# A graph network of two layers on one core: the order of the attention matmuls, their row halves, and the banks of the values behind attention

## The chip, the cores and the metric

The kernel runs on 1 core of one Trainium2 chip. The metric is the device time in microseconds (us) of one execution. TensorE (PE) multiplies matrices with an array of 128 by 128; PSUM is the memory that it writes. VectorE (DVE), ScalarE (ACT) and GpSimd (POOL) work element by element, and SyncE (SP) issues most of the DMAs. Each engine works through its own queue in the order in which its instructions were issued.

## What is computed

Both layers of the network see 8 batches of 2048 nodes with 256 features, all in fp32. Layer 0 is attention in chunks of 256 keys, with the softmax inside each chunk; layer 1 is a graph attention over all nodes. Shortened:

```
h = relu(layernorm(x))
q, k, v = h @ Wq.T + bq, h @ Wk.T + bk, h @ Wv.T + bv      # 4 heads of 64
scores = clip(q . k / sqrt(64), -10, 10), by chunks of 256 keys
scores = where(mask == 0, -10, scores)
ctx = sum over chunks of softmax(scores over the chunk) @ v
x = x + layernorm(ctx @ Wo.T + bo + h) * gamma + beta

h = relu(layernorm(x));  g = h @ W
e = leaky_relu(g @ a1 [rows] + g @ a2 [columns]), -1e9 where adj == 0
x = x + relu(softmax(e) @ g)
```

## The kernel before, in words

**Stages of a batch.** A batch has 4 blocks of 512 nodes, called zero, low, mid and last. Its attention has 32 steps, one for each block of 512 queries and chunk of 256 keys. After them come the rest of the output of layer 0 for the last blocks, the values of layer 1 (`Between.values`, line 843: g and the two scores of each node, from the features `hT`) and the products of layer 1 (`Layer1.products`, line 994). The next batch's q and k (`ahead.qk`, line 447) are made for its first block in steps 32 and 33 of this one, the rest behind attention. Attention of the next batch starts within the last layer-1 products (`early`, lines 581 to 603).

**A step of attention.** The logits of a step are made in four units (`logits`, line 503). A unit is one of the four heads: `ORDER` on line 485 maps a unit to a pair of heads and a row half of the array, the rows 0 to 63 or 64 to 127. Units 0 and 2 work on the upper half (the second 64 rows), units 1 and 3 on the lower. A matmul has 64 rows and 32 columns, so eight of them fit into the array at a time if both halves are used, four if one is. A unit has two halves of four matmuls each, one for each tile of 128 keys (`kt`).

After the logits, VectorE clips and masks a unit (`clip`, line 543), and ScalarE takes the exponential (`exponentials`, line 552). GpSimd adds the two key tiles of a pair of heads (`add`, line 558) into a tile tagged "both", of which there are two buffers. From these the sums of the softmax are made with ones as weights (`sums`, line 531, into ps_t), upper half first and lower half later; the values (`values`, line 519, into two ps_n banks) take the exponentials themselves, half of their matmuls in a first group and half in a later one, one step later. ScalarE inverts the sums (`invert`, lines 563 and 564), VectorE scales the values (`scale`, line 573), and a DMA that GpSimd issues adds the result to the context (`gather`, line 578). Two groups that write one bank of PSUM from different row halves must not run together, so a `fence` (a nop on SyncE, line 475) stands between them: the second waits for a signal that SyncE gives when the first has ended. As SyncE's queue is in order, a DMA behind such a nop is issued after it.

**The order.** It is written by hand (the engines are scheduled manually): `begin(f)` and `end(f)` issue step f, f from 2 to 34, with work from four steps: later values of step f-3, inversion and scale of f-3, logits of f-1, first values and sums of f-2, and the first unit of f. At set half steps (`todo`, keys 2f and 2f+1) other work is called in between: pieces without a mark, and pieces marked "first", "pe", "pe1" or "after" at other places of the step. Half step 65 has the four DMAs that send the turned features of block low (`low.send1`, line 143), half step 67 their fetch (`low.fetch1`, line 155). Half steps 66 and 67 have, for the next batch, q and k of the first block; in the last batch there is no next one, and the values of block zero and the first sources and weights of layer 1 (lines 843, 961 and 971) take their place.

In the kernel before, TensorE's order in `end(f)` and `begin(f)`, f within a batch, is:

```
begin: later values(f-3) | logits(f-1) units 1 and 2
end:   first values(f-2) | unit 3 of f-1 beside upper sums(f-2) | rest of unit 3 beside unit 0 of f
       | lower sums(f-2) beside the rest of unit 0 of f
```

where "beside" means on the other row half. In `early(3)` the first unit of step 1 stands without such a partner. At the end of a batch `last_sums` (in `end(33)`) ends the last step with values and sums mixed.

**PSUM.** It has 2 buffers of two banks (ps_s), 2 of one bank (ps_n) and 2 of one bank (ps_t). ps_s holds logits, ps_n values, ps_t sums. `ps_h` gives one half of a ps_s; `ps_m` gives ps_t, or ps_n and ps_t in turn when `turn_about` says so. Behind the last step the four values of block low go to `ps_h`. Each is copied out by ScalarE (line 851) and VectorE (line 852), and the third needs the buffer of the first.

Of the kernel before, what the change touches and what calls it, by code (L numbers as in the profile page):

```python
# [28 lines left out]
def gnn_two_layers(  # L29
# [29 lines left out]
    KT = CHUNK // P  # L59
# [18 lines left out]
    turn_about = [False, 0]  # L78
# [394 lines left out]
    def fence(before, after):  # L473

        nop = nc.sync.nop()  # L475
        for x in before:
            tc.add_manual_dep(nop.ins, x.ins.name, SYNC, reason="both write one bank of PSUM")
        for x in after:
            tc.add_manual_dep(x.ins, nop.ins.name, SYNC, reason="both write one bank of PSUM")


    class Attention:
# [100 lines left out]
        def early(self, part):  # L583

            if part == 0:
                for kt in range(KT):
                    self.logits(0, 0, kt)
                    self.logits(0, 1, kt)
            elif part == 1:
                for o in range(2):  # L590
                    self.clip(0, o)
                    self.exponentials(0, o)
                for kt in range(KT):
                    self.logits(0, 2, kt)
                    self.logits(0, 3, kt)
            elif part == 2:
                self.clip(0, 2)
                self.exponentials(0, 2)
                self.clip(0, 3)
                self.add(0, 0)  # L600
            if part == 3:
                for kt in range(KT):
                    self.logits(1, 0, kt)

# [3 lines left out]
        def begin(self, f, pieces=()):  # L610

            self.run(pieces, "first")
            if (f - 3, 0) in self.before:
                made = {}
                for kt in range(KT):
                    for half, c in ((0, 0), (1, 1)):
                        made.setdefault(c, []).extend(self.values(f - 3, half, c, kt))
                for c in range(2):
                    fence(self.before.pop((f - 3, c)), made[c])
            if (f - 1, 0) in self.s:  # L620
                self.clip(f - 1, 0)
            if self.has(f - 3):
                self.invert(f - 3)
            if self.has(f - 2):
                self.exponentials(f - 2, 3)
            if self.has(f - 1):
                self.exponentials(f - 1, 0)
            if self.has(f - 3) and not self.has(f - 1):
                self.scale(f - 3, 0)
                self.scale(f - 3, 1)  # L630
            self.run(pieces, "pe")
            if self.has(f - 1):
                for kt in range(KT):
                    self.logits(f - 1, 1, kt)
                    self.logits(f - 1, 2, kt)
                if self.has(f - 3):
                    self.scale(f - 3, 0)
                    self.scale(f - 3, 1)
            if self.has(f - 2):
                self.add(f - 2, 1)  # L640
            if self.has(f - 3):
                self.gather(f - 3)
            self.rest = pieces

        def end(self, f, pieces=()):
            self.run(pieces, "first")
            if self.has(f - 1):
                self.clip(f - 1, 1)
            self.run(pieces, "pe1")
            if self.has(f - 1):  # L650
                self.clip(f - 1, 2)
            self.run(pieces, "after")
            self.run(self.rest, None)
            if self.has(f - 1):
                self.exponentials(f - 1, 1)
                self.exponentials(f - 1, 2)
            if self.has(f - 2):
                made = {}
                for kt in range(KT):
                    for half, c in ((0, 1), (1, 0)):  # L660
                        made.setdefault(c, []).extend(self.values(f - 2, half, c, kt))
                for c in range(2):
                    self.before[f - 2, c] = made[c]
            if self.has(f - 1):
                self.logits(f - 1, 3, 0)
            if self.has(f - 2) and self.has(f - 1):
                sums = self.sums(f - 2, 1)
            if self.has(f - 1):
                self.logits(f - 1, 3, 1)
            if self.has(f):  # L670
                self.logits(f, 0, 0)
            self.run(pieces, None)
            self.run(pieces, "pe")
            if self.has(f - 2) and self.has(f - 1):
                fence(sums, self.sums(f - 2, 0))
            elif self.has(f - 2):
                self.last_sums(f - 2)
            if self.has(f):
                self.logits(f, 0, 1)
            if self.has(f - 1):  # L680
                self.clip(f - 1, 3)
                self.add(f - 1, 0)

        def last_sums(self, n):

            upper = self.sums(n, 1)
            made = {0: self.values(n, 0, 0, 0), 1: self.values(n, 1, 1, 0)}
            made[0] += self.values(n, 0, 0, 1)
            lower = self.sums(n, 0)
            made[1] += self.values(n, 1, 1, 1)  # L690
            for c in range(2):
                fence(self.before.pop((n, c)), made[c])
            fence(upper, lower)

        @staticmethod
        def run(pieces, kind):
# [5 lines left out]
    class Between:  # L702
# [148 lines left out]
            nc.scalar.activation(g[:, at, 0:F], pp[:, 0:F], AF.Copy)  # L851
            nc.vector.tensor_copy(self.sd[:, :, at], pp[:, F:F + 2])

        def ends(self, part):

            if part == 0:
                self.turn1(0)
                self.keep1(0)
                self.turn1(1)
                self.keep1(1)  # L860
            else:
                for t in range(TB):
                    self.values(t)
                    self.keep(t)

        def beside(self, soon):
# [300 lines left out]
    for b in range(B):  # L1167
        sd = small.tile([P, 2, NT], F32, tag="sd", name="sd", bufs=2)
        sums = small.tile([P, NNB, FC], F32, tag="sums", name="sums", bufs=2)
        blocks = [Between(nb, projs[b], att, sd, sums) for nb in range(NNB)]  # L1170
        zero, low, mid, last = blocks
# [24 lines left out]
        if b == 0:  # L1196
# [4 lines left out]
            for nb, ns in enumerate(beats):  # L1201
# [3 lines left out]
                n = ns[-1]  # L1205
# [40 lines left out]
                    piece()  # L1246
        for f in range(2, STEPS + 3):
            if f == STEPS + 2:
                turn_about[:] = [True, 1]
            att.begin(f, todo.pop(2 * f, []))  # L1250
            if unfinished:
                unfinished()
                unfinished = None
            att.end(f, todo.pop(2 * f + 1, []))
# [5 lines left out]
        if ahead:  # L1260
            for t in range(TB):
                mid.stats1([t])
                low.values(t, ps_h)
                low.keep(t)
            low.sum1()
            zero.fetch1()
# [60 lines left out]
            ahead.values(3)  # L1327
        else:
            one.weights(0, 0, range(2, 4), ws[0])
            low.ends(1)  # L1330
            low.sum1()
            one.send(1)
            mid.stats1(range(TB))
# [1 line left out]
            mid.shift1()  # L1335
            accs[0] = one.accumulators(0)
            early(0)
            mid.norm1(0)
            mid.norm1(1)
# [20 lines left out]
            for t2 in range(2):  # L1360
                last.gamma(t2)
                last.add(t2)
            early(1)
            last.stats1(range(TB))
            last.power1()
            last.shift1()
            weights(3)
            last.norm1(0)
            last.norm1(1)
            early(2)  # L1370
            last.ends(0)
            one.total()
# [56 lines left out]
        if ahead:  # L1429
            def unfinished(one=one, acc=accs[NNB - 1]):  # L1430
                one.finish(NNB - 1, acc)
                one.store(NNB - 1)
# [30 lines left out]
```

## Time and profile before

| | |
|---|---|
| time, median of 3 runs | 3520.11 us (3519.66 to 3520.38) |
| profiled execution, its time | 3520.81 us |
| its span | 3519.0 us, granted TensorE clock 1.00 |
| longest groups: clips (L543, VectorE) | 1024 of 1221 ns |
| adds (L558, GpSimd) | 512 of 2419 ns |
| logits (L503, TensorE) | 16384 records of 590 ns, busy 1334.4 us together |
| values (L519, TensorE) | 16384 records of 589 ns, 1120.4 us |
| sums (L531, TensorE) | 4096 records, 548.5 us |
| exponentials (L552, ScalarE) | 1024 of 1049 ns |
| scale (L573, VectorE) | 448 of 687 ns |
| products of layer 1 (L994, TensorE) | 4096 records of about 380 ns |

The span is the time from the first to the last instruction of one profiled execution. A row of a timeline has its start, its duration, the engine, the line of the kernel, the operation, and what is written from what; x32 at its end means that 32 instructions in a row are drawn together. In square brackets stands how long the engine was idle ahead of it, and what it waited for. A matmul in fp32 gives two records, so the 8 matmuls of a unit are 16 records. Records overlap where they work on different tiles of the array, so a busy sum can exceed what the array could do, and a busy TensorE is not a full one. One batch to the next takes 433.9 us (the products' first row in the chain is at 893.25 and then 1327.15).

### The profile page before, as it was taken

Reading aid. Unit: us, or ns where it says so; the run is one execution under the profiler, and the core shown is the slowest. Engines: PE = TensorE matmul, PEld = TensorE weight load, DVE = VectorE, ACT = ScalarE, POOL = GpSimd, SP = SyncE. Lnnn points to the kernel's source line nnn. Section 1 sums busy time; section 2 is a strip of 40 time slices with the busy share of each in tenths; the row PEclk is TensorE's granted clock in tenths of the full one; section 3 lists DMA queues with packets and bytes.
Section 4 is the critical chain, followed back from the end, with each engine's and each line's share of the span. In section 5 each row is a group of like instructions: output and inputs, shape, how many; then the busy total and the mean of one; then the engine's idle time right before and its main releaser. Section 6 shows DMA issues by size and latency. Waiting matters only on the chain.

```text
span 3519.0 us, 104592 instructions
## 1 busy us (share of the span) xinstructions
PE 3499.1 (99%) x46076; PEld 2302.1 (65%) x46076; DVE 2629.9 (75%) x3983; ACT 1959.0 (56%) x2961; POOL 1825.4 (52%) x1198
## 2 busy tenths in 40 slices
PE   9999999999999999999999999999999999999999
PEld 5454775667765577566876758656686655864568
DVE  6887677867678676786767867678686785857876
ACT  6777426763267633676336763367623776147751
POOL 5677017870278702786037850378503784047841
PEclk9999999999999999999999999999999999999999
DMA  7545323443234431444314443244432335124331
GB/s 246 127 109 123 93 88 72 97 108 104 69 86 86 116 102 61 92 92 109 102 61 92 92 105 101 67 92 87 117 106 64 79 85 122 64 55 92 80 77 53
DMA packets 171320, 332.13 MB, mean 94 GB/s; under 512 B 28656, under 2 KB 90352, under 8 KB 170864
## 3 DMA queue, kind: packets, MB, share of 16 engines
q1 hardware_dynamic: 129712, 205.36, 18.5%
q0 software_dynamic: 32832, 119.03, 18.5%
q8 instruction: 360, 5.90, 0.7%
q10 hardware_dynamic: 8320, 1.05, 0.2%
q14 instruction: 96, 0.79, 0.1%
HBM read 156.50 MB, written 51.44 MB: 59 GB/s over the span
## 4 chain that ended last, share of the span: by engine, by line
PE 98%; DVE 1%; ACT 1%; DMA 0%; issue 0%; POOL 0%; SPq 0%; ACTq 0%; DVEq 0%; POOLq 0%
PE ps_s L503 25%; PE ps_n L519 25%; PE ps_s L994 13%; PE ps_t L531 6%; PE ps_n L994 6%; PE ps_t L994 6%; PE ps_t L743 2%; PE ps_t L447 2%; PE ps_n L447 2%; PE ps_s L447 2%; PE ps_n L461 2%; PE ps_t L461 2%; PE ps_n L843 1%; PE ps_t L843 1%; PE ps_s L843 1%; PE ps_n L721 0%
## 5 line engine op out<-in xcount | busy, mean ns | idle before, releaser
L543 DVE SCALAR_TENSOR_TENSOR e<-ps_s,bound 128x1024 f32<-128x1024 f32 x1024 | 1219.2, 1221 | 400.9 <-PE ps_s L503 395.7
L558 POOL TENSOR_TENSOR both<-e 128x1024 f32<-128x1024 f32 x512 | 1222.3, 2419 | 541.9 <-PE ps_t L531 244.7
L503 PE MATMUL ps_s<-q,k 64*32 64x512 f32 x16384 | 1334.4, 590 | 0.2
L552 ACT ACTIVATE e<-e 128x1024 f32<-128x1024 f32 x1024 | 1049.4, 1049 | 456.0 <-DVE e L543 438.3
L519 PE MATMUL ps_n<-e,v 64*32 64x512 f32 x16384 | 1120.4, 589 | 0.0
L503 PEld LDWEIGHTS ps_s<-q,k 64*32 64x32 f32 x16384 | 505.0, 106 | 403.0 <-issue 277.9
L519 PEld LDWEIGHTS ps_n<-e,v 64*32 64x32 f32 x16384 | 522.5, 107 | 365.3 <-issue 266.4
L531 PE MATMUL ps_t<-both,ones 64*32 64x512 f32 x4096 | 548.5, 590 | 0.0
L994 PE MATMUL ps_s<-g,w 128*128 128x257 f32 x2048 | 448.4, 380 | 0.0
L994 PEld LDWEIGHTS ps_s<-g,w 128*128 128x128 f32 x2048 | 388.4, 190 | 56.0
L573 DVE TENSOR_TENSOR prod<-ps_n,rz 128x512 f32<-128x512 f32 x448 | 288.7, 687 | 135.4 <-ACT rz L564 86.5
L1017 POOL TENSOR_TENSOR x<-x,r 128x256 f32<-128x256 f32 x124 | 90.7, 745 | 459.5 <-ACT r L1015 458.7
L977 DVE SCALAR_TENSOR_TENSOR w<-bound,w 128x1024 f32<-128x1024 int8 x256 | 314.7, 1229 | 8.7
L367 POOL TENSOR_TENSOR krn<-krn,mv 128x4 f32<-128x4 f32 x28 | 6.8, 242 | 571.0 <-DVE w L971 571.0
L994 PE MATMUL ps_n<-g,w 128*128 128x257 f32 x1024 | 292.4, 382 | 0.0
L994 PE MATMUL ps_t<-g,w 128*128 128x257 f32 x1024 | 289.7, 380 | 0.0
L563 ACT ACTIVATE rz<-ps_t 128x512 f32<-128x512 f32 x256 | 152.6, 596 | 237.5 <-PE ps_t L531 164.2
L971 DVE TENSOR_SCALAR w<-src,cd 128x512 f32<-128x512 f32 x512 | 263.3, 556 | 19.2 <-ACT src L951 15.3
L994 PEld LDWEIGHTS ps_n<-g,w 128*128 128x128 f32 x1024 | 192.8, 190 | 44.3 <-issue 17.6
L578 POOL DMA_DIRECT2D ctxT<-prod x224 | 192.3, 858 | 56.5 <-DVE prod L573 49.5
L531 PEld LDWEIGHTS ps_t<-both,ones 64*32 64x32 f32 x4096 | 151.9, 106 | 100.6 <-SPq L475 44.4
L994 PEld LDWEIGHTS ps_t<-g,w 128*128 128x128 f32 x1024 | 193.8, 189 | 28.2
(139 smaller groups left out, 2975.8 us busy)
## 6 DMA issues: line engine op xcount, KB each, us to landing
ctxT<-prod POOLq DMA_DIRECT2D x224, 512.0 KB, 5.0
bound<-bound_d SPq DMA_DIRECT2D x125, 512.0 KB, 4.7
turned_d<-squares SPq DMA_DIRECT2D x232, 128.0 KB, 2.9
hT<-turned_d SPq DMA_DIRECT2D x58, 512.0 KB, 4.6
rows<-in_adj_dram SPq DMA_DIRECT2D x32, 512.0 KB, 5.2
x<-in_x_dram SPq DMA_DIRECT2D x32, 512.0 KB, 6.5
out_dram<-x SPq DMA_DIRECT2D x31, 512.0 KB, 2.7
xp<-in_x_dram SPq DMA_DIRECT2D x28, 512.0 KB, 4.4
```

Source lines behind the costliest of these rows:

```text
L447: nc.tensor.matmul(in_key_order(pp) if i == 0 else pp, w[:, di, do * P:(do + 1) * P], h, start=di == 0, stop=di == FC - 1,)
L503: nc.tensor.matmul(self.s[n, o][c * Q:(c + 1) * Q, kt, :], self.k[p][rows, at:at + Q], self.q[p][rows, nb * NB:(nb + 1) * NB], start=True, ...
L519: made.append(nc.tensor.matmul(self.num[n, c][h * Q:(h + 1) * Q, :], self.v[rows, j * KT + kt, at:at + Q], self.e[n, p][rows, i * KT + kt, :],
L531: nc.tensor.matmul(self.total[n][h * Q:(h + 1) * Q, :], ones[rows, :], self.both[n, h // 2][rows, h % 2, :], start=half == 1, stop=half == 0,)
L543: nc.vector.scalar_tensor_tensor(self.e[n, p][:, i * KT:(i + 1) * KT, :], self.s.pop((n, o)), -CLIP * SC, bounds[nb, j // 4][:, j % 4 * KT ...
L552: nc.scalar.activation(e, e, AF.Exp, scale=1.0 / SC)
L558: nc.gpsimd.tensor_tensor(self.both[n, p], e[:, 0], e[:, 1], op=ALU.add)
L573: nc.vector.tensor_tensor(dst[:, c, :], self.num.pop((n, c)), self.rz[n], op=ALU.mult)
L578: nc.gpsimd.dma_start(self.ctxT[nb], self.prod.pop(n), accum_op=ALU.add)
L971: nc.vector.tensor_scalar(w[:, i, :], self.src[nb], self.cd[:, 0, j:j + 1], self.cd[:, 1, j:j + 1], op0=ALU.mult, op1=ALU.max,)
L977: nc.vector.scalar_tensor_tensor(two, bounds1[nb, j // 8][:, j % 8 - 1:j % 8 + 1, :], 0.0, two, op0=ALU.is_gt, op1=ALU.mult)
L994: nc.tensor.matmul(accs[t][:, 0:F + 1], w[:, i, t * P:(t + 1) * P], g[:, j, :], start=j == 0, stop=j == NT - 1,)
```

## The change

The units of a step are now made in the order 1, 0, 3, 2, and those of the next step start before this one is done, a unit sooner than before: within a batch a step has, in this order,

```
begin: later values(f-3) | logits(f-1) units 3 and 2
end:   first values(f-2) | unit 1 of f beside upper sums(f-2) | rest of unit 1 beside unit 0 of f
       | lower sums(f-2) beside the rest of unit 0 of f
```

`early(3)` makes units 1 and 0 of step 1, on both halves, and their clip, and `early(2)` has one exponential more. In step 32, which has no next step, the sums and first values of step 30 stand in `begin` ahead of the rest of unit 2; in step 33 the sums and first values of 31 stand ahead of the pieces of the step (k of the next batch, or the sources of layer 1) and the later values behind them. `sums_and_values` puts upper sums, first values and lower sums in a row; `last_sums` is gone. Behind the last step, two of the four values of block low go to ps_h and two to ps_t; in the last batch all four get their banks by name (ps_t, ps_t, ps_n, ps_n), and `turn_about` starts at 0 in place of 1.

```diff
             if part == 2:
...
                 self.clip(0, 3)
+                self.exponentials(0, 3)
                 self.add(0, 0)
             if part == 3:
                 for kt in range(KT):
+                    self.logits(1, 1, kt)
                     self.logits(1, 0, kt)
+                self.clip(1, 1)
...
     def begin(self, f, pieces=()):
...
+                self.later_values(f - 3)
...
-            if self.has(f - 3):
+            if (f - 3) in self.total:
                 self.invert(f - 3)
-            if self.has(f - 2):
-                self.exponentials(f - 2, 3)
             if self.has(f - 1):
+                self.exponentials(f - 1, 1)
                 self.exponentials(f - 1, 0)
-            if self.has(f - 3) and not self.has(f - 1):
+            if self.has(f - 3) and not self.has(f):
                 self.scale(f - 3, 0)
                 self.scale(f - 3, 1)
             self.run(pieces, "pe")
             if self.has(f - 1):
-                for kt in range(KT):
-                    self.logits(f - 1, 1, kt)
-                    self.logits(f - 1, 2, kt)
+                self.logits(f - 1, 3, 0)
+                self.logits(f - 1, 2, 0)
+                self.logits(f - 1, 3, 1)
+            if self.has(f):
+                self.logits(f - 1, 2, 1)
...
             if self.has(f - 2):
                 self.add(f - 2, 1)
+            if self.has(f - 1) and not self.has(f):
+                self.sums_and_values(f - 2)
+                self.logits(f - 1, 2, 1)
...
     def end(self, f, pieces=()):
-                self.clip(f - 1, 1)
+                self.clip(f - 1, 3)
...
-                self.exponentials(f - 1, 1)
+                self.exponentials(f - 1, 3)
                 self.exponentials(f - 1, 2)
...
+            if self.has(f):
+                self.first_values(f - 2)
+                self.logits(f, 1, 0)
+                sums = self.sums(f - 2, 1)
+                self.logits(f, 1, 1)
+                self.logits(f, 0, 0)
+                self.run(pieces, None)
+                self.run(pieces, "pe")
+                fence(sums, self.sums(f - 2, 0))
+                self.logits(f, 0, 1)
+                self.clip(f, 1)
+            else:
+                last = self.has(f - 2) and not self.has(f - 1)
+                if last:
+                    self.sums_and_values(f - 2)
+                self.run(pieces, None)
+                if last:
+                    self.invert(f - 2)
+                self.run(pieces, "pe")
+                if last:
+                    self.later_values(f - 2)
             if self.has(f - 1):
                 self.add(f - 1, 0)

+        def sums_and_values(self, n):
+            sums = self.sums(n, 1)
+            self.first_values(n)
+            fence(sums, self.sums(n, 0))
...
             if f == STEPS + 2:
-                turn_about[:] = [True, 1]
+                turn_about[:] = [True, 0]
...
-                low.values(t, ps_h)
+                low.values(t, ps_h if t < 2 else ps_t)
...
-            low.ends(1)
+            low.ends(1, [ps_t, ps_t, ps_n, ps_n])
```

More of the change, by code (lines that the diff above doesn't have):

```diff
@@ L613, in begin @@
             if (f - 3, 0) in self.before:
-                made = {}
-                for kt in range(KT):
[L616 to L619, printed above, removed]
+                self.later_values(f - 3)
             if (f - 1, 0) in self.s:
                 self.clip(f - 1, 0)
-            if self.has(f - 3):
+            if (f - 3) in self.total:
                 self.invert(f - 3)
-            if self.has(f - 2):
-                self.exponentials(f - 2, 3)
             if self.has(f - 1):
+                self.exponentials(f - 1, 1)
                 self.exponentials(f - 1, 0)
-            if self.has(f - 3) and not self.has(f - 1):
+            if self.has(f - 3) and not self.has(f):
                 self.scale(f - 3, 0)
@@ L632, in begin @@
             if self.has(f - 1):
-                for kt in range(KT):
-                    self.logits(f - 1, 1, kt)
-                    self.logits(f - 1, 2, kt)
+                self.logits(f - 1, 3, 0)
[3 more added lines that the diff above has]
+                self.logits(f - 1, 2, 1)
                 if self.has(f - 3):
@@ L654, in end @@
             if self.has(f - 1):
-                self.exponentials(f - 1, 1)
+                self.exponentials(f - 1, 3)
                 self.exponentials(f - 1, 2)
[L657 to L663, printed above, removed]
-            if self.has(f - 1):
-                self.logits(f - 1, 3, 0)
@@ L666, in end @@
[L666 to L679, printed above, removed]
@@ L680, in end @@
-            if self.has(f - 1):
-                self.clip(f - 1, 3)
-                self.add(f - 1, 0)
[L684 to L690, printed above, removed]
+            if self.has(f):
[19 more added lines that the diff above has]
+                    self.later_values(f - 2)
@@ new lines, in end, with first_values @@
+            if self.has(f - 1):
+                self.add(f - 1, 0)
+        def sums_and_values(self, n):
+            sums = self.sums(n, 1)
+            self.first_values(n)
+            fence(sums, self.sums(n, 0))
+        def first_values(self, n):
+            made = {0: [], 1: []}
+            for kt in range(KT):
+                for half, c in ((0, 1), (1, 0)):
+                    made[c] += self.values(n, half, c, kt)
+            for c in range(2):
+                self.before[n, c] = made[c]
@@ L691, in last_sums, with later_values @@
+        def later_values(self, n):
+            made = {0: [], 1: []}
+            for kt in range(KT):
+                for half, c in ((0, 0), (1, 1)):
+                    made[c] += self.values(n, half, c, kt)
             for c in range(2):
                 fence(self.before.pop((n, c)), made[c])
-            fence(upper, lower)
         @staticmethod
@@ L852, in keep, with ends @@
             nc.vector.tensor_copy(self.sd[:, :, at], pp[:, F:F + 2])
-        def ends(self, part):
+        def ends(self, part, banks=()):
             if part == 0:
@@ L862, in ends @@
                 for t in range(TB):
-                    self.values(t)
+                    self.values(t, *banks[t:t + 1])
                     self.keep(t)
```

## Prediction

> **What bounds the kernel.** I read the page first, then the waits of all engines, then the timeline of the change of batch after batch 0, engine by engine.
>
> ```profile
> span 3519.0 us, 104592 instructions
> PE 3499.1 (99%) x46076; PEld 2302.1 (65%) x46076; DVE 2629.9 (75%) x3983; ACT 1959.0 (56%) x2961; POOL 1825.4 (52%) x1198
> PE 98%; DVE 1%; ACT 1%; DMA 0%; issue 0%; POOL 0%; SPq 0%; ACTq 0%; DVEq 0%; POOLq 0%
> ```
>
> TensorE is busy 99% and carries 98% of the chain that ended last. But busy does not mean full: a matmul of 64 rows uses half of the array. So I ask where only one half works. These are two rows of TensorE in a last layer-1 stretch, then its rows in the change of batch:
>
> ```profile
> 936.91 1.95 PE L503 MATMUL ps_s<-q,k 64*32 64x512 f32 x32
> 945.92 1.92 PE L503 MATMUL ps_s<-q,k 64*32 64x512 f32 x16
> ...
> 766.60 0.61 PE L503 MATMUL ps_s<-q,k 64*32 64x512 f32 x4
> 766.81 0.72 PE L531 MATMUL ps_t<-both,ones 64*32 64x512 f32 x4
> ...
> 767.46 1.04 PE L503 MATMUL ps_s<-q,k 64*32 64x512 f32 x8
> 768.31 0.61 PE L531 MATMUL ps_t<-both,ones 64*32 64x512 f32 x4
> 768.34 0.63 PE L519 MATMUL ps_n<-e,v 64*32 64x512 f32 x4
> 768.74 0.61 PE L531 MATMUL ps_t<-both,ones 64*32 64x512 f32 x4
> ...
> 782.87 2.01 PE L843 MATMUL ps_s<-w1s,hT 128*128 128x258 f32 x8
> 786.31 2.01 PE L843 MATMUL ps_s<-w1s,hT 128*128 128x258 f32 x8 [1.43 <-DVE sd L852]
> 788.16 1.89 PE L461 MATMUL ps_t<-wvT,hT 128*128 128x256 f32 x8
> ```
>
> Each fp32 matmul is two records. 32 records on both halves take 1.95 us (1.72 from start to start in the steady rows), 16 on one half 1.92: half of the array is lost, 0.86 us of full work. At 767.46 unit 3's second half (8 records, 0.86 to the next group) stands alone on one half. From 784.38 to 786.31 the values of block 1 wait for the copy L852 on VectorE. In a steady step of batches 1 to 7 I find no such hole: the starts of the values repeat every 7.73 us (753.72, 761.45), and 72 matmuls at 16 in 1.72 us are 7.74.
>
> **The steady steps: nothing.** In a steady step the new order is the old with the names changed: later values 16 matmuls, logits of two units 16, first values 16, then 24 in which each group of four meets one of the other half, one unit's logits beside the upper sums, one of the next step beside the lower. The clips, adds, inversions, scales and fences come at the same distances. Only two exponentials (1.05 us each) come a unit earlier, so first values have more slack; but no value waited for ACT there, so that slack buys nothing. 31 steps x 8 batches: 0 us. Batch 0's waits for clips held up behind VectorE's adjacency work stay where they are.
>
> **Early in layer 1.** Unit 1 of step 1 joins the lone unit 0 on the idle half: 8 matmuls (16 records) at no time, since 16 and 32 records take the same 1.9 us. The gain shows at step 32, which has 56 matmuls of attention in place of 64: 0.86 us. One more clip (1.22) there lies on VectorE between weights, beside layer-1 products that have 4 tiles in hand; bounds 0 to +0.2 per batch, I take 0.
>
> **Step 32, in u = us from the start of the later values of 29 (761.45 before).** Before, it took u 0 to 9.55 up to q of the next batch (771.00). After:
> - later values(29) to 1.72, unit 3 beside the first half of unit 2 to 2.57, the rest of unit 3 to 3.43, and now the upper sums of 30. They read what GpSimd adds:
>
> ```profile
> 761.80 4.76 POOL L558 TENSOR_TENSOR both<-e 128x1024 f32<-128x1024 f32 x2 [0.84 <-PE ps_t L531]
> ```
>
> - These adds start when the lower sums of 29 have freed the buffer (u 0.35) and end at 5.11; nothing in the change moves that. Before, the upper sums came at 5.36, with first values ahead of them. After, nothing else is left for the upper half from 2.57, for the lower from 3.43: both stand till about 5.17, as all later matmuls are queued behind the halted weight load (batch 0 has such a hole already: 150.08 to 150.73, both halves idle). Then upper sums 0.86, first values(30) 1.72, lower sums beside unit 2's second half 0.86: to 8.6. Without the halt it would be 6.0 (1.72 + 0.86 + 0.86 + 1.72 + 0.86). The halt costs 2.6 us; bounds 0, if the adds were early enough, and 3.4, if nothing of the lone unit 3 ran beside it.
> - Does a hole cost more than itself? The Trainium skill, "TensorE: Matmul & The Clock Gate", section "Why this matters for your kernels", asks for no idle gaps over about 3 us, after which the clock falls to half for a while. The nearest row is the windows' row of the stretch with the 1.43 us hole:
>
> ```profile
> 783.00:788.20 5.20, 3.77 (x17) 2.97 (x18) 2.44 (x9) 2.27 (x5) 2.24 (x3) 1.00 0.44 113
> ```
>
> Its columns are the stretch and its length, busy us (and instructions) of PE, PEld, DVE, ACT and POOL, then the granted clock, which stays 1.00, DMA share and GB/s. By row and rule 1.74 us of a wholly idle array adds nothing; if it tripped the gate, one window of some 3.4 us at half rate would be an estimate of 1.7 more per change. I take 0.
> - SyncE. The fence of the sums now stands ahead of block 1's four sends, which at 761.00 took 2.70 us with nothing in front. Fence near 6.2, sends to about 9.1, then the two fences of later values(30): they start near 9.4 where TensorE could at 8.7. Cost 0.7 (bounds 0 to 1.5; the sends' longest issue in a change of batch is near 3.5).
> - later values(30) to 11.1, q to 14.8. ScalarE meanwhile: clip of unit 2 to 10.1, its exponential 11.2, residual 12.2, inversion (0.60+0.63) 13.4, scale on VectorE 14.7, which frees the bank of first values(31): no wait beyond q's own end. Sums and values of 31 (2.58) to 17.4, k 3.63 to 21.0, later values(31) 1.72 to 22.7.
>
> **The values of block 1.** Two now go to ps_t: no wait for the copies. 8 groups of 0.43 us, 3.46, in place of 5.29 (782.87 to 788.16): 1.83 gained, to 26.2. Before they ended at 26.7. So a change of batch gains 1.83 here, 0.86 by the 8 matmuls, 0.9 where unit 3 and the lower sums no longer stand alone on one half, and 0.3 around k (sums and first values 2.58 and later values 1.72, before 1.88 and 2.73), and pays 2.6 (halt) and 0.7 (sends): 3.9 less 3.3, where the two ends (26.2 and 26.7) give -0.5, which I take. Bounds -1.2 and +0.5; were the halt and the sends free it would be -3.8, which is the rival below. The other bank takers behind attention alternate the other way round (the turn starts at 0 in place of 1) and find a free bank either way: 0. Five batches -0.5 each, one with long sends 0.
>
> **The fetch of block 1.** On SyncE it passes the fence of the sums of 31.
>
> ```profile
> 761.00 2.70 SPq L143 DMA_DIRECT2D turned_d<-squares  x4
> 768.33 1.68 SPq L155 DMA_DIRECT2D hT<-turned_d  x2
> 781.38 0.34 SPq L178 DMA_DIRECT2D bound<-bound_d  x1
> ```
>
> It was issued at u 6.9; now after the upper sums of 31, u 15.9, behind the gather of 30 that moves until 19. The DMA view of that window has 6.1 us from issue to landing, the page 4.6: it lands at 20.5 to 22.0, needed at 22.7. Cost 0, with 0.7 us to spare. In batch 0 a further send stands before it (3.5 us): lands near 24, +0.8.
>
> **The last batch.** Step 33 has the values of block 0 in place of q and k, in the two ps_s banks. The third waits for a copy behind inversion and scale of 30 (+1.0). Sources and first weights of layer 1 now wait for the lower sums of 31, and scale(31), which frees ps_n for the last two values of block 1, comes after them: u 24.7, products (line 994) at 26.5; before at 23.46 (3388.84 - 3365.38). +3.0, bounds 0 and +5.
>
> **Sum.** 0 + 5 x (-0.5) + 0 + 0.8 + 3.0 = +1.3 on the profiled execution's 3520.8 (span 3519.0 and 1.8 around it); its median is 0.7 lower, so 3520.1 + 1.3 = 3521.4. Bounds of this case: 7 x (-1.2) + 3.0 = -5.4 and 7 x 0.5 + 0.8 + 3.0 = +7.3, so 3515 and 3527. That the change in effect does nothing (3520) lies inside.
>
> **Rivals.** *Faster*: the halt does not bind, because the exponentials that come a unit earlier let GpSimd add earlier. Then the sends end near 7.4, later values(30) start at 7.7 in place of 9.4, and the chain to first values(31) moves with them: 1.7 us x 8 = 13.6, to 3508; if the sends cost nothing either, 3503. For it: the wait is the only large loss of the change. Against: the row at 761.80 names the sums as what GpSimd waited for, not an exponential. *Slower, one mechanism*: the fetch of block 1 on SyncE lands late. It decides from 6.8 us after its issue (22.7 - 15.9). For it: the gather shares the 16 DMA engines (the page has 5.0 us for it alone), and the fence makes the two meet. Against: the 6.1 us measured in this window already had such traffic. At 8.5 us, TensorE waits 1.7 in 7 changes: +12, 3533. The clock's 1.7 x 8 = 14, to 3535, counts within slower.
>
> **Numbers.** About 0.2% (7.0 us) is what a measurement of this kernel can tell from no change: limits 3513.1 and 3527.1. The likeliest case, net nothing, 0.49, own range 3515 to 3527; faster 0.22; slower 0.29, mostly to 3536. The range 3507 to 3536 leaves out some 0.1 on each side.
>
> **What would show it.** In each change of batch: line 531 waits for POOL line 558 for 1.7 to 2.6 us, a wait that before has no size there; no line 843 wait for L852; the sends after the fence, near u 6.2; the fetch near u 16; the period from batch to batch 433.9 less 0.5; the first line 994 of batch 7 some 3 us later against its later values(29). Wrong, if TensorE shows no hole ahead of the sums (faster), if line 843 waits for the DMA of hT (slower), or if a steady step is not 7.73 us, which would mean that the orders are not alike.

## The result and the profile after

The changed kernel takes 3532.4 us (median of 7 runs, 3530.75 to 3532.8), before 3520.11: slower by 12.3 us. The ratio on record is 1.0032, with a 95% interval of 1.0023 to 1.0042 (the two medians alone give 1.0035). The forecast was 3521.4 with a range of 3507 to 3536; the likeliest case said no net change, and the 12 us lie in the case that had 0.29. The profiled execution took 3530.91 us, 10.1 more than that of before. The three page lines that answer to those shown of before:

```profile
span 3529.1 us, 104629 instructions
PE 3496.9 (99%) x46076; PEld 2304.4 (65%) x46076; DVE 2621.2 (74%) x3983; ACT 1960.0 (56%) x2961; POOL 1826.0 (52%) x1198
PE 95%; POOL 1%; DVE 1%; SPq 1%; ACT 1%; issue 0%; DMA 0%; POOLq 0%; DVEq 0%; ACTq 0%
```

The totals say little: TensorE is even 2.2 us less busy in a span 10.1 us longer. So the time went into holes. Where, is read from the longest row of the products of layer 1 in each batch, the one of 128 records, in the chain of both traces (the rows at 893.25 and 1327.15, by which a batch before takes 433.9 us, are these; they are not the first of the products):

| row of 128 records of line 994 (after: 1003) in batch | before | after | added since the row above |
|---|---|---|---|
| 0 | 459.35 | 462.04 | 2.69 |
| 1 | 893.25 | 896.59 | 0.65 |
| 2 | 1327.15 | 1331.70 | 1.21 |
| 3 | 1761.05 | 1766.31 | 0.71 |
| 4 | 2195.00 | 2201.13 | 0.87 |
| 5 | 2628.90 | 2635.66 | 0.63 |
| 6 | 3062.80 | 3070.51 | 0.95 |
| end of the span | 3519.0 | 3529.1 | 2.39 |

(The chain gives the rows of batches 0 to 6; the last line holds all of batch 7.) Each batch pays. (Batch 2 adds 0.5 us more than batch 1, though its change of batch takes no longer: 27.39 us from the later values of step 29 to the end of the values of block low, 27.34 after batch 1. The rest lies in its attention; why is open.) Within a batch the steady steps are as before: the later values of steps 28 and 29 start at 756.44 and 764.16, 7.72 us apart. The change of batch after batch 1 on TensorE, with u 0 at 764.16 (block 1, here and below, is the block called low above):

```profile
767.39 0.60 PE L531 MATMUL ps_t<-both,ones 64*32 64x512 f32 x2
769.27 0.62 PE L531 MATMUL ps_t<-both,ones 64*32 64x512 f32 x2 [1.28 <-POOL both L558]
...
771.49 1.41 PE L503 MATMUL ps_s<-q,k 64*32 64x512 f32 x6
774.12 1.98 PE L519 MATMUL ps_n<-e,v 64*32 64x512 f32 x32 [1.23 <-SPq L475]
776.03 3.70 PE L447 MATMUL ps_s<-hT,wqT 128*128 128x512 f32 x8
...
782.40 3.70 PE L447 MATMUL ps_s<-hT,wkT 128*128 128x512 f32 x8
786.03 1.95 PE L519 MATMUL ps_n<-e,v 64*32 64x512 f32 x32
787.91 2.01 PE L852 MATMUL ps_s<-w1s,hT 128*128 128x258 f32 x8
789.75 1.91 PE L852 MATMUL ps_t<-w1s,hT 128*128 128x258 f32 x8
791.50 1.89 PE L461 MATMUL ps_n<-wvT,hT 128*128 128x256 f32 x8
```

There are two new holes: 1.28 us within the sums of 30, for GpSimd's adds, and 1.23 us at the later values of 30 (774.12), for a fence on SyncE. Both stand in all eight batches; the second is longest in batch 0:

```profile
339.24 1.98 PE L519 MATMUL ps_n<-e,v 64*32 64x512 f32 x32 [2.44 <-SPq L475]
```

The hole of 1.43 us in the values of block 1 is gone: line 852 runs through from 787.91 to 791.50. SyncE in the same stretch:

```profile
770.49 3.52 SPq L143 DMA_DIRECT2D turned_d<-squares  x4
780.98 1.60 SPq L155 DMA_DIRECT2D hT<-turned_d  x2
```

The four sends begin at u 6.33, after the fence of the sums, and take 3.52 us to issue, to 774.01; the later values start 0.1 us after that. Before, the sends were issued at u -0.4 and were long done.

### The profile page after: what moved, and what is told of

The parts are those of the page before. It is cut to its first block, busy times and chain, and to the rows that moved or that the text cites. A ratio compares the mean times of both kernels' runs of the same rounds, so it can differ in the third digit from the quotient of the medians.

```text
span 3529.1 us, 104629 instructions
## 1 busy us (share of the span) xinstructions
PE 3496.9 (99%) x46076; PEld 2304.4 (65%) x46076; DVE 2621.2 (74%) x3983; ACT 1960.0 (56%) x2961; POOL 1826.0 (52%) x1198
## 4 chain that ended last, share of the span: by engine, by line
PE 95%; POOL 1%; DVE 1%; SPq 1%; ACT 1%; issue 0%; DMA 0%; POOLq 0%; DVEq 0%; ACTq 0%
PE ps_s L503 24%; PE ps_n L519 24%; PE ps_s L1003 12%; PE ps_n L1003 6%; PE ps_t L1003 6%; PE ps_t L531 6%; PE ps_t L752 2%; PE ps_n L447 2%; PE ps_t L447 2%; PE ps_s L447 2%; PE ps_n L461 2%; PE ps_t L461 1%; PE ps_t L852 1%; PE ps_n L852 1%; POOL both L558 1%; SPq L143 1%
## 5 line engine op out<-in xcount | busy, mean ns | idle before, releaser
L519 PE MATMUL ps_n<-e,v 64*32 64x512 f32 x16384 | 1132.0, 589 | 11.6 <-SPq L475 11.6
L531 PE MATMUL ps_t<-both,ones 64*32 64x512 f32 x4096 | 553.3, 590 | 10.1 <-POOL both L558 9.4
L531 PEld LDWEIGHTS ps_t<-both,ones 64*32 64x32 f32 x4096 | 143.0, 105 | 100.9 <-SPq L475 38.4
```

Source lines behind the costliest of these rows:

```text
L519: made.append(nc.tensor.matmul(self.num[n, c][h * Q:(h + 1) * Q, :], self.v[rows, j * KT + kt, at:at + Q], self.e[n, p][rows, i * KT + kt, :],
L531: nc.tensor.matmul(self.total[n][h * Q:(h + 1) * Q, :], ones[rows, :], self.both[n, h // 2][rows, h % 2, :], start=half == 1, stop=half == 0,)
```

## Experiments

Theory Q: the sends, moved behind the fence of the sums, hold back the fences of the later values of 30. Theory H: the halt at the sums costs the time. Theory F, the rival of the prediction: the fetch of block 1 lands late. All ratios below are to the kernel before, timed on the same chip; on the four chips used it took 3520.3 to 3520.9 us, so versions timed on different chips compare to within about half a us.

**1. The sends first.** In the changed kernel block 1's sends go ahead of the fence (all batches):

```diff
-            at(33, self.send1)
+            if self.nb == 1:
+                at(32, pe(lambda: self.send1()))
+            else:
+                at(33, self.send1)
```

> The four sends of block 1 stand one half step sooner, ahead of the fence of the upper sums of 30. Theory Q (the sends, held back by that fence on SyncE, hold back the fences of the later values of 30): these values start at u 8.8 in place of 10.0, first values of 31 are then held by the scale at u 14.6, so 0.9 us less per change of batch and about 2 in batch 0: 3532.4 - 8 = 3524. Theory H (only the halt at the sums counts): no change, 3532. Theory F (the fetch of block 1 lands late): no change, 3532.

3523.44 us, ratio 1.0007 (0.9999 to 1.0016): 9.0 us of the 12.3 are gone by moving four DMA issues. The change after batch 1 on TensorE (the view ends at 776.5) and on SyncE:

```profile
773.61 2.02 PE L519 MATMUL ps_n<-e,v 64*32 64x512 f32 x26
775.56 1.13 PE L447 MATMUL ps_s<-hT,wqT 128*128 128x512 f32 x2
```

```profile
764.80 3.40 SPq L143 DMA_DIRECT2D turned_d<-squares  x4
```

The sends run beside matmuls that do not wait for SyncE, and q starts at u 10.38 (775.56 less 765.18), 1.5 us sooner than the 11.87 above. That is more than the 0.9 expected: the later values start while the last logits still run on the other half, and first values of 31 need only the first of the two scales. In batch 0 the wait did not go, it moved: there the later values of 31 wait 2.20 us for their fence. Ahead of it on SyncE stand the two fetches, which are issued from 346.38 to 350.44, behind the sends of the next batch.

**2. First values ahead of the sums.** TensorE gets work while GpSimd adds:

```diff
-                self.sums_and_values(f - 2)
+                self.first_values(f - 2)
+                sums = self.sums(f - 2, 1)
+                fence(sums, self.sums(f - 2, 0))
                 self.logits(f - 1, 2, 1)
```

> First values of 30 ahead of the upper sums of 30 in step 32, so that TensorE has work while GpSimd adds. Theory Q: the upper sums run at the same time as before, so fence, sends and later values of 30 stay where they are; 0, 3532. Theory H: 1.8 us less per change of batch (unit 2 ends at u 6.9 in place of 8.7), eight times: 3518. Theory F: 3532.

3540.59 us, ratio 1.0057 (1.0044 to 1.0069): slower by 8 us, which no theory expected. The change after batch 1, and a row of the windows (length, busy PE, PEld, DVE, ACT, POOL, then the granted clock):

```profile
772.51 0.61 PE L503 MATMUL ps_s<-q,k 64*32 64x512 f32 x4
775.79 3.11 PE L519 MATMUL ps_n<-e,v 64*32 64x512 f32 x32 [2.67 <-SPq L475]
778.83 4.22 PE L447 MATMUL ps_s<-hT,wqT 128*128 128x512 f32 x8
```

```profile
775.70:779.00 3.30, 3.21 (x33) 0.90 (x34) 0.11 (x1) 1.99 (x4) 2.36 (x1) 0.62 0.43 109
```

Theory Q holds: the halt is gone, and yet the later values start at u 10.04 (775.79 less 765.75), as in the changed kernel at 9.96, held by the same fence behind the same sends. The halt had been hidden. What is new is that the two holes have become one of 2.67 us, and after it the granted clock is 0.62: the same 32 records take 3.11 us in place of 1.98, and q 4.22 in place of 3.70, 1.65 us together. Of the five whole batches that the chain gives from 463.62 to 2643.80, one has no such drop and takes 434.60 us, as a batch of the changed kernel; the others take 436.21 to 436.77. In all eight changes there are six drops: 6 x 1.65 = 9.9 us, and the profiled execution is 9.7 longer than that of the changed kernel (3540.59 and 3530.91).

**3. Both edits.**

> Both edits: sends ahead of the fence, and first values of 30 ahead of the sums. Theory Q with H as its second gate: later values of 30 start at u 7.0 in place of 10.0, first values of 31 at 12.7 behind the scale in place of 15.5: 2.8 us less, eight times, 3510. If the two losses simply add up: the sum of what the two edits give alone. Theory F: the fetch, issued sooner by the same 2.8 us, waits the same, 3532 or little less.

3511.97 us, ratio 0.9975 (0.9966 to 0.9984). The change after batch 1, with u 0 at 762.92:

```profile
770.07 1.93 PE L519 MATMUL ps_n<-e,v 64*32 64x512 f32 x32
771.93 3.70 PE L447 MATMUL ps_s<-hT,wqT 128*128 128x512 f32 x8
```

The later values of 30 start at u 7.15 with no hole ahead of them, and q at 9.01. Singly the edits gave -9.0 and +8.2, together -20.4: the two waits stand side by side, and what one saves is only had in full if the other is gone too. Theory F forecast little or nothing here.

**4. The banks alone,** put into the kernel before:

```diff
-                low.values(t, ps_h)
+                low.values(t, ps_h if t < 2 else ps_t)
...
-                turn_about[:] = [True, 1]
+                turn_about[:] = [True, 0 if ahead else 1]
```

> The kernel before with the new banks alone: the third and fourth values of block 1 to ps_t in seven changes of batch (the last batch as before). If the 1.8 us wait for the copies is gone and nothing takes its place: 3520.1 - 7 x 1.8 = 3507.3. If the wait only moves to later bank takers: 3520.

3514.85 us, ratio 0.9984 (0.9977 to 0.9991): 5.3 us gained where 12.8 were expected.

```profile
783.85 1.91 PE L843 MATMUL ps_t<-w1s,hT 128*128 128x258 f32 x8
785.59 1.89 PE L461 MATMUL ps_n<-wvT,hT 128*128 128x256 f32 x8
788.04 1.99 PE L461 MATMUL ps_t<-wvT,hT 128*128 128x256 f32 x8 [0.55 <-DVE sd L852]
```

The values no longer wait, but the second half of v does (0.55 us), for the copy that frees ps_t; that copy stands on VectorE behind the late scale of 31 and the statistics. A batch takes 433.0 us (458.48 to 891.50), 0.9 less than before where 1.8 were expected: half of the gain is handed back, most of it at the next taker of the bank.

**5. The banks and the last sums ahead of k,** in the kernel before, with the units in the old order; the last batch as before:

```diff
+            alone = self.has(f - 2) and not self.has(f - 1) and not self.final
+            if alone:
+                sums = self.sums(f - 2, 1)
...
+            if alone:
+                fence(sums, self.sums(f - 2, 0))
             self.run(pieces, None)
+            if alone:
+                self.invert(f - 2)
             self.run(pieces, "pe")
...
+            elif alone:
...
```

> The kernel before with the new banks and with the last sums ahead of k (upper sums, first values, lower sums of 31, then inversion, k, later values), in the seven batches that have a next one; units in the old order. Banks alone gave 3514.9, since the second group of v (line 461) then waited 0.55 us for a copy behind the late scale of 31. If the earlier sums bring the scale forward, that wait goes, and some 0.3 of matmuls alone on a half: 3514.9 - 7 x 0.85 = 3509. If the fetch, now behind the fence of these sums, comes too late: 3515 or more.

3510.33 us, ratio 0.9971 (0.9960 to 0.9981). A batch takes 432.2 us (766.55 to 1198.74 at first values of 30), before 433.9: 1.7 us, nearly all that the banks had promised.

```profile
786.39 1.91 PE L857 MATMUL ps_t<-w1s,hT 128*128 128x258 f32 x8
788.13 1.89 PE L461 MATMUL ps_n<-wvT,hT 128*128 128x256 f32 x8
789.86 1.89 PE L461 MATMUL ps_t<-wvT,hT 128*128 128x256 f32 x8
```

No wait at line 461. These two parts of the change pay together, so what makes it slower is among the rest; as the steady steps and layer 1 cost nothing (7.72 us a step; the end of experiment 12), that is the new step 32.

**6. The fetch of block 1 ahead of the fence of the sums of 31.**

```diff
-        at(STEPS2 + 3, low.fetch1)
+        at(STEPS2 + 2, pe(lambda: low.fetch1()))
```

> The changed kernel with the fetch of block 1 issued one half step sooner, ahead of the fence of the sums of 31, so that it has the lead that it had before. Theory Q (the sends and the fences behind them): only the 0.9 us that the last batch shows for it, 3531.5. Theory F (the fetch is what made the change slower): 1 to 2 us less in each change of batch, 3522 or below.

3532.2 us, ratio 1.0035 (1.0022 to 1.0047): nothing. Theory F falls. The changed kernel's trace says the same: in its first seven batches no row of line 852 waits for the fetch. The last batch's wait for this fetch (0.88 us in the changed kernel) is gone, and 0.92 us for the scale stand in its place at the next two values. In batch 4 a hole of only 1.64 us, 3.6 us after the end of one of 1.02, is followed by a clock of 0.78 and then 0.65:

```profile
2078.37 3.50 PE L519 MATMUL ps_n<-e,v 64*32 64x512 f32 x32 [1.64 <-SPq L475]
```

```profile
2077.00:2080.00 3.00, 1.63 (x24) 0.73 (x32) 1.00 (x1) 1.96 (x4) 2.24 (x2) 0.78 0.72 176
2080.00:2083.00 3.00, 3.00 (x27) 0.86 (x10) 1.14 (x2) 1.19 (x3) 1.58 (x1) 0.65 0.22 64
```

**7. Batch 0 alone.** Sends first in batch 0, and the fetch for the next batch's second block a step later there:

```diff
+            if self.nb == 1 and self.proj.b == 0:
+                at(32, pe(lambda: self.send1()))
...
-            at(STEPS2 + 3, pe(lambda: ahead.qk(0, 1, ps_h)), lambda: ahead.fetch(1))
+            at(STEPS2 + 3, pe(lambda: ahead.qk(0, 1, ps_h)))
+            at(STEPS2 + (4 if b == 0 else 3), lambda: ahead.fetch(1))
```

> The changed kernel with the sends of block 1 ahead of the fence in batch 0 alone, and with the fetch of the next batch's second block a step later there, so that it stands ahead of no fence. Theory Q: batch 0's hole of 2.4 us before the later values of 30 goes, about 2.0 less (3530.4 at most). Theory G (a hole of over 2 us lets TensorE's clock fall to half for some time in a part of the executions, 1.6 to 1.7 us each, and this is why the runs of the changed kernel fall into two groups, 3530.8 and 3532.5): one group remains, near 3529, with a spread below 1 us. Rival to G: the two groups come from something else, and two groups 1.7 apart remain.

3531.03 us, ratio 1.0029 (1.0018 to 1.0041): 1.4 less, not the 2.0 expected, and the runs still fall into two groups (3529.5 and 3529.7; 3530.8 to 3531.9). The hole moved on: block 1's fetch stands behind the sends of the next batch, as it does in the changed kernel, but now it is late,

```profile
352.83 3.67 PE L852 MATMUL ps_s<-w1s,hT 128*128 128x258 f32 x8 [2.63 <-DMA hT<-turned_d]
```

and those 8 matmuls take 3.67 us in place of 2.01. The profiled execution (3531.86) is the slowest of the upper group. So this does not decide on theory G: batch 0 still has a hole of over 2 us, and the one traced execution has a drop behind it. Here the late fetch of the rival does exist, in batch 0, once nothing in front of it is late.

**8. Step 33 of the last batch as before.** First values of 31, then sources and first weights of layer 1, then the last sums and later values mixed, and the old banks:

```diff
+                if last and self.final:
+                    self.first_values(f - 2)
+                    self.run(pieces, None)
+                    self.run(pieces, "pe")
+                    self.last_sums(f - 2)
+                    return
                 if last:
                     self.sums_and_values(f - 2)
```

> The changed kernel with step 33 and the banks of the last batch alone in the order of before (sources and first weights of layer 1 ahead of the last sums). By the trace the first product of layer 1 stands at u 25.9 in place of 23.5: 2.4 less, 3530.0, of which 0.9 by the fetch that no longer stands behind the fence. If the loss of the last batch lies in step 32 alone: 3532.4.

3530.96 us, ratio 1.0032 (1.0020 to 1.0045); its runs are three from 3530.6 to 3531.0 and two near 3533.4, so the median does not tell. The trace decides: the first product of layer 1 stands at 3398.99, in the changed kernel at 3398.94, with later values of 30 at 3383.09 and 3383.21. The kernel before agrees: counted from the later values of 29, the values of block zero start at u 9.55 there and at 12.03 in the changed kernel, and from there to the first product it is 13.91 and 13.82. The last batch's loss comes from step 32, as everywhere.

**9. All queues mended:** edits 1, 2 and 6 together, and the fetch for the next batch a step later in every batch.

> The version with sends first and values first, and both fetches moved as well: block 1's ahead of the fence of the sums, the next batch's a step later. Against that version's 3512.0: batch 0 showed 2.1 us of waiting on SyncE ahead of the later values of 31, and the last batch a late fetch (up to 2 us): 3508.5. If these waits are only handed on: 3512.

3508.07 us, ratio 0.9965 (0.9952 to 0.9979), the fastest version, 12 us ahead of the kernel before. A batch takes 431.75 us (764.24 to 1195.99).

**10. And step 33 of the last batch as before** (edits 8 and 9).

> The version with all queues mended (3508.1) with step 33 and the banks of the last batch in the order of before. In the changed kernel that order was worth nothing, as the last batch lost its time in step 32. Here step 32 is mended, and the values of block 1 still show a wait of 0.9 us for the scale of 31 in the last batch: if the order of step 33 costs anything, it shows here as up to 0.9 us, 3507.2; if not, 3508.1. (The wait of 1.4 us for the copies in step 33 is in both.)

3509.45 us, ratio 0.9969 (0.9958 to 0.9980). From first values of 30 to the first product the last batch takes 21.16 us (3355.01 to 3376.17), in version 9 20.99. The order of step 33 is worth nothing here either.

**11. Unit 2's second half beside unit 3's,** in version 9: the sums of 30 then stand alone.

```diff
-            if self.has(f):
+            if self.has(f - 1):
                 self.logits(f - 1, 2, 1)
+            if self.has(f):
...
                 fence(sums, self.sums(f - 2, 0))
-                self.logits(f - 1, 2, 1)
```

> The version with all queues mended (3508.1), and in step 32 both halves of unit 2 beside those of unit 3; the sums of 30 then stand alone, the lower ones beside the later values of 30. If halves that stand alone are what is left there: 8 matmuls less on a lone half, 0.86 us in each batch, 3501.2. If the fences of the later values decide: 3508.

3509.9 us, ratio 0.9970 (0.9958 to 0.9981): not faster. A batch takes 432.0 us (767.62 to 1199.62), 0.25 more than in version 9; eight times that is about the 1.8 us between the two. The lone half has only changed its place, to upper and lower sums one after the other. The profiled execution was slower still (3512.92): in its setup, behind a hole of 2.79 us, the clock was at 0.78 from 54 to 60 us.

```profile
48.00:54.00 6.00, 3.21 (x14) 2.37 (x13) 3.51 (x6) 1.63 (x3) 3.38 (x4) 0.94 0.81 263
54.00:60.00 6.00, 6.00 (x66) 3.78 (x66) 3.44 (x6) 1.95 (x3) 1.60 (x3) 0.78 0.30 87
```

**12. Unit 1 of step 1 alone,** in step 2 of the changed kernel, and not beside unit 0 in layer 1:

```diff
             if part == 3:
                 for kt in range(KT):
-                    self.logits(1, 1, kt)
                     self.logits(1, 0, kt)
-                self.clip(1, 1)
...
+            if f == 2:
+                for kt in range(KT):
+                    self.logits(1, 1, kt)
+                self.clip(1, 1)
+                self.exponentials(1, 1)
```

> The changed kernel without the pairing in layer 1: unit 1 of step 1 is made alone in step 2, as 16 records on one half. If those matmuls were free beside unit 0 in layer 1, they now cost 1.72 us in each batch when nothing runs beside them, 3532.4 + 13.8 = 3546, and 0.86 when the other half is filled, 3539. If pairing is worth nothing: 3532.

3560.85 us, ratio 1.0112 (1.0097 to 1.0128): 28.4 us more than the changed kernel, twice the most expected. The lone unit takes its 1.7 us, and then units 2 and 3 wait for its bank:

```profile
526.24 2.78 PE L503 MATMUL ps_s<-q,k 64*32 64x512 f32 x24
529.50 1.92 PE L503 MATMUL ps_s<-q,k 64*32 64x512 f32 x24 [0.49 <-DVE e L543]
530.96 1.06 PE L519 MATMUL ps_n<-e,v 64*32 64x512 f32 x8
```

From 526.24 to first values it takes 4.72 us; in the changed kernel the same stretch is 1.74 (523.75 to 525.49). That is 3.0 of the 3.8 us that a batch is longer (464.56 to 902.93, 438.4, against 434.6). So most of this loss is the wait for a bank, not the lone matmuls. That they are free beside unit 0 in layer 1, the changed kernel shows itself, where the row of 16 records in 1.92 us has become

```profile
514.71 1.95 PE L503 MATMUL ps_s<-q,k 64*32 64x512 f32 x32
```

## Why the prediction was right or wrong

**The total: inside the range, by luck.** 3532.4 lies within 3507 to 3536, but outside the 3515 to 3527 of the case that was called likeliest, and the two mechanisms named for a slower result, the late fetch and the clock, did not make the 10.1 us of the two profiled executions. Two terms of the likeliest case's own sum did, which were sized too small and count again in every batch.

**Steady steps, nothing: right,** 7.72 us a step. **Early in layer 1, free: right** (the row at the end of experiment 12). The clip there cost nothing that can be seen.

**The halt at the sums: its time was right, its price was not.** It was predicted to end at u 5.17 and unit 2 at 8.6; measured 5.11 and 8.7. (The earlier hole that the prediction cites for it, at 150.08, is only a gap between starts: four logits that began at 150.06 run through it.) But 2.6 us were booked for the halt and 0.7 more for the sends, as if each could be had back alone. Experiments 1 to 3 show two paths, from GpSimd's adds over TensorE and over SyncE, which meet at the later values of 30, and the later one counts: q started at u 11.87; moving the sends alone brought it forward by 1.5 us, taking the halt away alone did nothing for these values (and added drops of the clock), both together brought q forward by 2.9.

**The sends: the term that was mis-sized.** The prediction took the 2.70 us of the row at 761.00 and had the later values start at u 9.4; the sends took 3.52 and the values started at 9.96, 0.56 later. In batch 0 they took 4.73 (334.39 to 339.12), and the values waited 2.44 us; booked was only the fetch, 0.8. Why the sends take longer is open: they took 3.40 also in experiment 1, ahead of the fence.

**The groups behind: the other mis-sized term.** Groups that change from one shape of matmul to another were counted at the steady 1.72 us for 16 matmuls. Measured from start to start: later values of 30 1.91, sums and values of 31 2.74 (counted at 2.58), later values of 31 1.88, values of block 1 3.59 (counted at 3.46). That is 0.64 more. The prediction's own figures of before had 1.88 and 2.73 around k, so the 0.3 that it hoped to gain there was not to be had. With the 0.56, the values of block 1 end at u 27.34 in place of 26.2; before it was 26.7. So the change after batch 1 came out at +0.65 and not at -0.5, and the others at +0.63 to +1.21.

**The banks: right in the changed kernel** (no wait at line 852), and only there: by themselves they give half (experiment 4), since the wait moves to v. That the last sums ahead of k are what keeps it away (experiment 5) was not in the prediction.

**The last batch: right in size (+3.0 predicted, +2.4 measured), wrong in cause.** It was put down to the order of step 33; experiments 8 and 10 find nothing there. The wait of 1.0 us for a copy did not come: the values of block zero run through from 3385.12 to 3388.96. In versions 9 and 10, where step 32 is shorter, it is there, with 1.40; so it is likely that the late step 32 hid it.

**The rival of the late fetch: wrong.** Its total (3533) is near the measured one by chance. The fetch was issued at u 16.8 and needed at 23.75, and nothing waited for it but in the last batch (0.88 us); experiment 6 shows that it is not the cause.

**The clock: its rule was wrong, its size right.** The prediction said that holes like these add nothing, by the row at 1.43 us and by the bound of about 3 us in the Trainium skill, "TensorE: Matmul & The Clock Gate", section "Why this matters for your kernels". Experiments 1, 2, 6 and 7 show the matmuls slow after holes of 2.20, 2.67, 1.64 and 2.63 us, at 1.6 to 1.7 us a time, which is the size that the prediction gave one drop; the measurement decides against the bound. In the profiled execution of the changed kernel no such drop is seen in the changes of batch, not even behind batch 0's 2.44 us, so the clock has no part in its 10.1 us. Its seven runs lie at 3530.8 (three) and 3532.4 to 3532.8 (four), about one drop apart, and the profile fell among the three. This fits, but no trace of the upper group was taken, and experiment 7 left a hole in batch 0, so it stays likely and not shown.

**The sum,** on the profiled executions: predicted +1.3; batch 0 +1.9 more, six changes +7.5 more, the last batch 0.6 less, which makes +10.1. The medians are 12.3 apart; of the 2.2 us more, one drop of the clock would be 1.65.

## What to carry to other kernels

A DMA issue is an instruction on a queue: if a fence is moved ahead of it on SyncE, the DMA waits with the fence, and the next fence waits for the DMA. Before reordering the work, list what stands on the queue between the fences, and move the issues to where nothing waits behind them. And test two waits that end at the same point together: one alone may seem worth nothing, as here, where two edits of -9 and +8 made -20.

## What the runs showed of the hardware

The granted clock of TensorE fell after five of the seven holes of 2.60 to 2.67 us in experiment 2, after its one of 3.62, after single ones of 2.63, 2.49 and 2.20 (experiments 7, 12 and 1), and once after 1.64 with another of 1.02 just before (experiment 6). It stayed at 1.00 after the other two of experiment 2 (2.65 and 2.66), after 2.44 in the changed kernel and after 2.10 in experiment 3, both in batch 0, where the next 32 records took 1.98 and 1.99 us. In stretches of 2 us it reads down to 0.50. A drop cost about 1.65 us, once 2.87 (experiment 12, batch 4). So in these runs the length of one hole does not decide, and a run can have one drop more or less: in experiments 5 and 11 one lay in the setup. Issuing the four sends of block 1, of 128 KB each, took from 2.55 us (before, batch 5) to 4.73 us (batch 0 of the changed kernel) of SyncE's time.
